# Region attention with keys on partitions, heads in pairs of array tiles, and row maxima only in a branch

## Chip, cores and metric

One core of one Trainium2 chip. The metric is the device time of one execution in microseconds (us), the median of several. A run is fast if it lies within 1.5% of the fastest of its kernel, and only fast runs are compared.

## The reference, cut to what matters

The input is `x`, 4 x 128 channels x 128 x 128. A first layer cuts each image into 9 x 9 overlapping regions of 16 x 16 pixels (step 14) and runs attention with 4 heads of 32 channels within each, then a depthwise 5x5 conv; a second layer has two quantised 3x3 convs. The change touches the attention and the layernorms:

```python
y = _ln(tok, ln1_g, ln1_b)                 # tok: regions x 256 tokens x 128
q, k, v = split(y @ w_qkv)                 # 4 heads of 32
attn = softmax(einsum('bhqd,bhkd->bhqk', q, k) * hd ** -0.5)
o = einsum('bhqk,bhkd->bhqd', attn, v)
tok = o @ w_out + b_out + tok
# overlapping regions are averaged into xf, then
y = _ln(xf, ln2_g, ln2_b) @ w_p0 + b_p0    # 128 -> 256
ym = depthwise_5x5(y); batchnorm; gelu ...
```

## The kernel before

A band is one row of nine regions; there are 36. While band t's attention runs, closures for the projections and second layernorm of band t-1, the first layernorm of band t+1 and the depthwise conv of band t-2 are placed between its steps. A scheduler then orders the instructions of each engine before the run. Scores have queries on partitions: DVE finds row maxima, ACT exponentiates and sums, POOL multiplies by the reciprocal sums, PE transposes, ACT copies, and PE multiplies by the values. Everything in this layer is fp32.

```python
def scores(u):                                   # u: one head of one region
    sc = ps_s.tile([P, 2, NT], F32)
    for c in range(2):
        matmul(sc[:, c, :], qk[hs, 0, c*P:(c+1)*P], qk[hs, 1, :])
    vector.tensor_reduce(nmax, sc, AX.X, ALU.max, negate=True)
    for c in range(2):
        scalar.activation(pr[:, c, :], sc[:, c, :], AF.Exp, bias=nmax[:, c:c+1], accum_out=den[:, c:c+1])
    vector.reciprocal(rden, den)
    for c in range(2):
        gpsimd.tensor_scalar(pr[:, c, :], pr[:, c, :], rden[:, c:c+1], 1.0, ALU.mult, ALU.mult)
def flip(u):    # 4 transposes into pt, then scalar.copy(prt, pt)
def values(u):
    for kc in range(2):
        matmul(po[hs, :], v[:, kc, hs], prt[:, kc, :], start=(kc == 0), stop=(kc == 1))
# step s: scores(s); flip(s - 2); values(s - 3)     39 steps in a band
# ...
side = post_steps(t - 1) if t >= 1 else []          # projections, layernorm 2
side += ln1_steps(t + 1) if t + 1 < T else []       # layernorm 1 of the next band
interleave(attention(t), side, conv_steps(t - 2) if t >= 2 else [])
```

## Time and profile before

| | before |
|---|---|
| median of 3 runs | 7746.85 us (7741.2 to 7783.33) |
| PE / DVE / ACT / POOL busy share of the span | 96 / 68 / 44 / 34% |
| attention stage, then the rest | about 6474 us, then about 1267 us |
| granted PE clock, mean | 0.980 |

The prediction below shows the lines. A busy share says how long an engine worked, not that the span depends on it; here both hold for PE, which is busy 98% of the steady part of the attention stage. The attention stage ends where the second layer's projection starts its first matmul. The "steady part" in this document runs from 360 us to 280 us before that end; the fences show stretches with round ends near it. "Lost clock" is the sum, over the stretches of the steady part in which the profile's clock record grants less than full speed, of their length times the share withheld, whether PE works then or stands. Before it is 73 us.

### The profile page before, as it was taken

What the parts mean: (1) busy time and instruction counts of PE and PEld (TensorE: products, weight loads), DVE (VectorE), ACT (ScalarE), POOL (GpSimd) and SP (SyncE); (2) the same over time, 40 slices, a digit from 0 to 9 for tenths busy, and PEclk for the clock granted to TensorE, in tenths of its full rate; (3) what the DMA queues carried; (4) which work ended last, traced back from release to release, by engine and by line L of the source; (5) the groups of instructions that cost most, each with busy time, mean ns of one, the idle gap of its engine ahead of it and who ended that gap; (6) DMA issues with size and microseconds to landing.
All of it is one profiled execution on the core that took longest, in us unless ns stands there. A gap on an engine that the chain in (4) does not pass through costs nothing.

```text
span 7740.7 us, 86177 instructions
## 1 busy us (share of the span) xinstructions
PE 7448.0 (96%) x28736; PEld 3798.7 (49%) x28736; DVE 5270.3 (68%) x7739; ACT 3438.1 (44%) x8922; POOL 2665.6 (34%) x3443
## 2 busy tenths in 40 slices
PE   8999999999999999999999999999999976999999
PEld 4555555554555555545555555455555532444444
DVE  3467777777677777776777777767777787663333
ACT  4544444443444444434444444444444414661123
POOL 2344444443444444434444444334444411110000
PEclk9999999999999999999999999999999987999999
DMA  0000000000000000000000000000000005870028
GB/s 27 16 28 20 22 20 24 22 24 23 20 20 29 20 22 20 24 22 20 24 22 29 20 22 21 24 20 22 25 22 24 14 23 181 283 245 1 1 78 266
DMA packets 160315, 347.05 MB, mean 45 GB/s; under 512 B 18177, under 2 KB 23937, under 8 KB 155265
## 3 DMA queue, kind: packets, MB, share of 16 engines
q1 hardware_dynamic: 159872, 341.54, 12.6%
q8 instruction: 231, 3.78, 0.2%
q14 instruction: 212, 1.73, 0.1%
HBM read 173.70 MB, written 167.77 MB: 44 GB/s over the span
## 4 chain that ended last, share of the span: by engine, by line
PE 84%; DVE 7%; POOL 4%; ACT 3%; issue 1%; DMA 0%; SPq 0%; DVEq 0%; POOLq 0%; ACTq 0%
PE pm L319 17%; PE sc L390 15%; PE po L430 14%; PE pc L521 10%; PE pt L415 7%; PE pm L372 5%; PE pm L282 4%; DVE acc L330 4%; PE pm L177 3%; PE pm L184 3%; PE pb L569 3%; PE pm L377 2%; PE pm L261 2%; POOL pr L405 2%; POOL xn L192 2%
## 5 line engine op out<-in xcount | busy, mean ns | idle before, releaser
L330 DVE SCALAR_TENSOR_TENSOR acc<-y,dwk,acc 128x1024 f32<-128x1024 f32 (+3 forms) x2736 | 3112.0, 1141 | 21.5
L405 POOL TENSOR_SCALAR pr<-pr,rden 128x256 f32<-128x256 f32 x2592 | 1992.5, 781 | 3086.6 <-DVE rden L403 2368.4
L390 PE MATMUL sc<-qk 32*128 32x256 f32 x5184 | 1467.8, 402 | 14.3 <-ACT pr L398 14.1
L419 ACT COPY prt<-pt 128x512 f32<-128x512 f32 x1296 | 762.4, 588 | 1472.7 <-PE pt L415 1457.9
L319 PE MATMUL pm<-y,diag 128*128 128x512 f32 (+1 forms) x3456 | 1375.5, 551 | 24.9 <-DVE acc L323 24.9
L430 PE MATMUL po<-prt,v 128*32 128x256 f32 x5184 | 1343.9, 388 | 22.4 <-ACT prt L419 22.3
L398 ACT ACTIVATE pr<-sc,nmax 128x256 f32<-128x256 f32 x2592 | 1206.8, 474 | 233.2 <-DVE nmax L394 156.9
L390 PEld LDWEIGHTS sc<-qk 32*128 32x128 f32 x5184 | 860.5, 185 | 778.5 <-issue 367.1
L394 DVE TENSOR_REDUCE nmax<-sc 128x2 f32<-128x512 f32 x1296 | 884.6, 683 | 467.0 <-PE sc L390 461.2
L521 PE MATMUL pc<-q,wq 128*128 128x512 fp8e4 x4608 | 1051.6, 380 | 13.8 <-issue 4.6
L319 PEld LDWEIGHTS pm<-y,diag 128*128 128x128 f32 x3456 | 648.6, 191 | 690.8 <-issue 642.1
L415 PE MATMUL pt<-ident,pr 128*128 128x128 f32 x5184 | 859.0, 286 | 29.0 <-POOL pr L405 25.0
L415 PEld LDWEIGHTS pt<-ident,pr 128*128 128x128 f32 x5184 | 568.6, 141 | 405.6 <-issue 256.7
L521 PEld LDWEIGHTS <-wq 128*128 128x128 fp8e4 x4608 | 447.9, 97 | 648.5 <-issue 157.0
L430 PEld LDWEIGHTS po<-prt,v 128*32 128x32 f32 x5184 | 457.4, 109 | 595.6 <-issue 143.6
L374 ACT COPY qk<-pm 128x512 f32<-128x512 f32 x324 | 189.7, 586 | 1035.7 <-PE pm L372 1035.7
L403 DVE RECIPROCAL rden<-den 128x2 f32<-128x2 f32 x1296 | 209.4, 162 | 600.1 <-ACT pr L398 555.5
L398 ACT ACTIVATION_READ_ACCUMULATOR pr<-sc,nmax 128x1 f32 x2592 | 530.1, 205 | 0.0
L323 DVE SCALAR_TENSOR_TENSOR acc<-y,dwk,pm 128x512 f32<-128x512 f32 (+1 forms) x288 | 197.6, 686 | 407.1 <-PE pm L319 407.1
L372 PE MATMUL pm<-yr,wqkv 128*128 128x256 f32 x1296 | 382.7, 410 | 37.7 <-POOL yr L192 37.7
L282 PE MATMUL pm<-xn,wp 128*128 128x512 f32 (+1 forms) x576 | 299.6, 648 | 31.5 <-POOL xn L192 22.5
L569 PE MATMUL pb<-ge,wp 128*128 128x512 f32 x512 | 253.3, 599 | 68.9 <-ACT ge L566 68.9
(86 smaller groups left out, 5032.1 us busy)
## 6 DMA issues: line engine op xcount, KB each, us to landing
cv<-cv_d SPq DMA_DIRECT2D x128, 512.0 KB, 4.3
cv_d<-acc SPq DMA_DIRECT2D x80, 512.0 KB, 2.9
xt<-in_x_dram SPq DMA_DIRECT2D x36, 1024.0 KB, 5.1
xfl<-xf_d SPq DMA_DIRECT2D x128, 256.0 KB, 3.2
id_d<-y SPq DMA_DIRECT2D x128, 256.0 KB, 2.6
idt<-id_d SPq DMA_DIRECT2D x128, 256.0 KB, 3.2
out_dram<-z SPq DMA_DIRECT2D x128, 256.0 KB, 2.5
xf_d<-xf SPq DMA_DIRECT2D x112, 256.0 KB, 2.0
```

The lines of the kernel that those rows point to most:

```text
L282: nc.tensor.matmul(pm[:, : n * P], wp0[:, h, :], held["xn"][:, : n * P], start=True, stop=True)
L319: nc.tensor.matmul(pm[:, :n, :], diag[:, h, k, :], tap(h, k, r, n), start=(k == 0), stop=(k == PE_TAPS - 1),)
L330: nc.vector.scalar_tensor_tensor(a, tap(h, k, g, gn), dwk[:, h, k : k + 1], a, ALU.mult, ALU.add)
L372: nc.tensor.matmul(pq[:, m, :], wqkv[:, m * P : (m + 1) * P], y, start=True, stop=True)
L390: nc.tensor.matmul(sc[:, c, :], qk[hs, 0, c * P : (c + 1) * P], qk[hs, 1, :], start=True, stop=True)
L394: nc.vector.tensor_reduce(nmax, sc, AX.X, ALU.max, negate=True)
L398: nc.scalar.activation(pr[:, c, :], sc[:, c, :], AF.Exp, bias=nmax[:, c : c + 1], accum_out=den[:, c : c + 1],)
L405: nc.gpsimd.tensor_scalar(pr[:, c, :], pr[:, c, :], rden[:, c : c + 1], 1.0, ALU.mult, ALU.mult)
L415: nc.tensor.transpose(pt[:, kc, c * P : (c + 1) * P], pr[:, c, kc * P : (kc + 1) * P], ident)
L419: nc.scalar.copy(prt, pt)
L430: nc.tensor.matmul(po[hs, :], v[:, kc, hs], prt[:, kc, :], start=(kc == 0), stop=(kc == 1))
L521: nc.tensor.matmul(pc, w[:, t, :], q[:, k * RB + dy : k * RB + dy + RB, dx : dx + P], start=(t == 0), stop=(t == 8),)
```

## The change

Its intent: compute the scores transposed, so that the keys are on partitions and the exponentials are at once the operand of the values matmul. That removes the transposes and their copies. The sums over keys, now over partitions, come from a matmul with ones; the division goes to the output. Without row maxima the exponential needs a bound on the scores, so a flag is computed from the weights and a branch holds the general form with maxima (not taken for these inputs). Heads go in pairs, whose matmuls lie in different tiles of the PE array. Gains and biases of the layernorms are folded into weights.

```diff
+    with tc.If(flag > 0): front(False)
+    with Else: front(True)             # with row maxima
 def scores(u):                         # u: now a pair of heads
-    vector.tensor_reduce(nmax, ...); Exp with bias and accum_out; reciprocal; gpsimd.tensor_scalar x2
+    sc = ps_s.tile([P, 2, 2, NT], F32)
+    for c in range(2):
+        for a in range(2):             # two heads, two row tiles
+            matmul(sc[:, a, c, :], qk[hs, 1, c*P:(c+1)*P], qk[hs, 0, :])
+    scalar.activation(pr, sc, AF.Exp)                                  # 1024 elements
+    gpsimd.tensor_tensor(both, pr[:, :, 0, :], pr[:, :, 1, :], ALU.add)
-def flip(u): ...
 def values(u):
+    for c in range(2):
+        for a in range(2):             # two column tiles
+            matmul(po[hs, 0, :], v[:, c, hs], pr[:, a, c, :], start=(c == 0), stop=(c == 1))
+    for a in range(2):
+        matmul(po[hs, 1, :], ones[:, hs], both[:, a, :])
+    # after the second pair: rden = exp(-ln(sums)) on ACT, product and overlap add on DVE
 # layernorm tail
-    vector.tensor_tensor(xh, pc, rstd, ALU.mult); gpsimd.tensor_scalar(o, xh, g, bias, ...)
+    # in its head: vector.tensor_copy(xc, pc)
+    gpsimd.tensor_tensor(o, xc, rstd, ALU.mult)
 # q,k out of PSUM
-    scalar.copy(qk, pq)
+    vector.tensor_tensor(qk, pq, bqk broadcast, ALU.add)
 # steps of a band
-    scores(s); flip(s - 2); values(s - 3)      # 39 steps
+    scores(s); values(s - 1)                   # 19 steps
 # PSUM banks
-    ps_s 2 x 1, ps_t 2 x 1, ps_o 1, ps_m 3
+    ps_s 2 x 2, ps_o 2, ps_m 2
```

## The prediction

> **What bounds the kernel now.** I read four views in this order: the page's busy table and slices, the stretches, the groups by line with shapes kept apart, and the timeline of one stretch.
>
> ```profile
> span 7740.7 us, 86177 instructions
> PE 7448.0 (96%) x28736; PEld 3798.7 (49%) x28736; DVE 5270.3 (68%) x7739; ACT 3438.1 (44%) x8922; POOL 2665.6 (34%) x3443
> ...
> PE 84%; DVE 7%; POOL 4%; ACT 3%; issue 1%; DMA 0%; SPq 0%; DVEq 0%; POOLq 0%; ACTq 0%
> ```
>
> ```profile
> 360.00:6280.00 5920.00, 5792.02 (x22124) 3038.70 (x22124) 4372.56 (x6237) 2721.92 (x7749) 2460.38 (x3064) 0.99 0.06 22
> 6280.00:6480.00 200.00, 93.54 (x200) 43.17 (x198) 182.84 (x200) 16.58 (x22) 9.59 (x20) 0.69 0.11 40
> ```
>
> The columns of the stretches are busy us of PE, PEld, DVE, ACT and POOL, then the granted clock. In the attention stage (to about 6480 us) PE is busy 98% of the steady stretch, DVE 74%, ACT 46%, POOL 42%. Only the last 180 us of the stage belong to DVE, which finishes the depthwise conv there. The remaining 1260 us are stages that the change doesn't touch. So PE's time in the attention stage is what counts, and the first question is where it goes.
>
> ```profile
> L390 PE MATMUL sc<-qk 32*128 32x256 f32 x5184 | 1467.8, 402 | 14.3 <-ACT pr L398 14.1
> L430 PE MATMUL po<-prt,v 128*32 128x256 f32 x5184 | 1343.9, 388 | 22.4 <-ACT prt L419 22.3
> L415 PE MATMUL pt<-ident,pr 128*128 128x128 f32 x5184 | 859.0, 286 | 29.0 <-POOL pr L405 25.0
> ```
>
> ```profile
> 3006.86 0.66 PE L415 MATMUL pt<-ident,pr 128*128 128x128 f32 x4
> 3007.45 1.05 PE L430 MATMUL po<-prt,v 128*32 128x256 f32 x4
> 3008.43 1.13 PE L390 MATMUL sc<-qk 32*128 32x256 f32 x4
> 3009.48 0.66 PE L415 MATMUL pt<-ident,pr 128*128 128x128 f32 x4
> ...
> 167.76 1.14 PE L390 MATMUL sc<-qk 32*128 32x256 f32 x8
> ```
>
> Two things are to be seen. One head costs 3009.48 - 3006.86 = 2.62 us of PE when nothing else comes between (four transposes 0.59, four value records 0.98, four score records 1.05). An fp32 matmul is two records here: 2592 score matmuls make 5184. And the last line is the key to the change: where scores of two heads happen to stand together, x8 takes 1.14 us, as long as x4. In the single records there, the two heads start 13 ns apart and proceed in step, 0, 13, 320, 333, 535, 549, 751, 765 ns. Two row tiles really run side by side in fp32. Two value groups side by side do the same (0, 14, 240, 254, 456, 470, 672, 685 ns), but such starts are rare now: 10 pairs of score records and 99 of value records.
>
> **What the Trainium skill says.** "TensorEngine Tiling (Array Packing)", Key Properties: different tiles execute independently, and changing the tiling mode drains the engine. The trace agrees with both: the 13 ns starts, and a record spacing of 216 ns within a score group against 305 to 309 ns where the shape of the tile changes. "SBUF — State Buffer", Who interferes with whom: a VectorE instruction with two SBUF inputs and a GpSimd instruction that reads SBUF exclude each other, and the second waits for the whole of the first. The trace agrees: the normalisation of probabilities on POOL takes 478 ns alone and 1503 ns when it starts inside a depthwise tap. "GPSIMD Engine Reference", 3.1: a two-input fp32 add of 2048 elements takes 4497 ns on GpSimd. This trace has no large two-input POOL instruction, so I scale to 512 elements and estimate 1.17 us from that page. "ScalarE: Activation LUTs", What ACT_TABLE_LOAD costs: 0.833 ns an element. The trace agrees: copies of 256 and 512 take 378 and 586 to 588 ns.
>
> **The change on PE.** A pair of heads has 4 score matmuls (8 records) in two row tiles, so 4 slots: 320 + 216 + 216 + 305 = 1.06 us. Values are 4 matmuls and the sums by ones 2 more, 12 records in two column tiles, 6 slots: 240 + 4 x 216 + 309 = 1.41 us. Transposes are gone. The pair costs 2.47 us in place of 2 x 2.62 = 5.24. Counting from the start of each PE record to the next one's, the three groups now take 1393 + 1280 + 835 = 3508 us of the stage's 6453 (some waits and mixing included). New: 648 pairs x 2.47 = 1600. PE saves 1908 and needs 6453 - 1908 = 4545 us. The last number still holds the conv tail.
>
> **The change on ACT and POOL.** ACT loses the transposed copies (762), the read-outs of sums (530), the q,k copies (190) and 2592 exponentials (1207). It gains 648 exponentials of 1024 elements at about 1.01 us (588 + 512 x 0.83 ns), 655 us, and ln and exp of the sums, 324 x (0.38 + 0.42) = 260. It falls to some 1.7 ms, and is no bound. POOL loses 1992 us of normalisation and gains 648 adds of the two key halves, 1.17 us alone; the 224 large layernorm scalings become two-input, too. With the waits for the shared port I expect 1.8 to 2.4 ms, no bound either. A step of one pair takes about 7 us, and exp plus add need 3 to 4, which the lag of one step covers.
>
> **The change on DVE.** In the stage it is now busy: taps 3116 (the 2736 of one line), first taps 198, statistics 172, residual 99, overlap add 135, layernorm product 180, row maxima 885, reciprocals 209, together 4994. Removed: maxima, reciprocals and layernorm product, 1274. Added: copy of the centred values out of PSUM (224 x 0.68 + 64 x 0.42 = 180), q,k bias (324 x 0.69, the shape of the layernorm product, = 222), scaling of the output by the reciprocal sums (324 x 0.42 = 135). New: 4994 - 1274 + 537 = 4257. On top comes the shared port. A 128x1024 tap that no POOL instruction overlaps takes 1.277 us, the overlapped ones 1.333, and all the taps lose only 82 us now, because POOL's pieces are 0.48 us and some 0.24 us of one hides under the next tap's start. A POOL add of 1.17 us that slips in between two taps delays the next by about 0.93 us. Of the 648 + 288 two-input POOL instructions I let 600 fall so (560 us, rounded down to 550 with the rest ignored). DVE: 4257 - 82 + 550 = 4725 us, **more than PE's 4545**. So the bound goes over from PE to DVE.
>
> **The sum.** DVE can't be full throughout. The first two bands have no conv; at 84 us each ((4545 - 1452) / 36, 1452 being the conv matmuls) it idles some 120 us. In-order waits for PE and ACT, 1.7 ms in total today beside a full PE, I put at 200. The stage: 4725 + 120 + 200 = 5045, that is 1408 less than 6453. The fold of gains, the bound for the scores and the branch stand before the first layernorm and let nothing overlap: 40 us, a guess. 7747 - 1408 + 40 = 6380. One risk has a direction: the score tiles double, so the general PSUM pool falls from three buffers to two, and q,k and the centred values are now evacuated by the full DVE instead of ACT. For PE stalls that come back as DVE waits I add 70: **6450 us**.
>
> **The rivals.**
> - *Serial tiles.* If the heads of a pair don't overlap in the new order, a pair needs 8 + 12 records of 216 ns and two switches, 4.7 us: PE saves only 3508 - 648 x 4.7 = 460, remains the bound at about 6.0 ms, and the kernel takes some 7300 us. Against it: the in-step starts above, and that the built program alternates heads within each group.
> - *PSUM starvation.* With two buffers PE waits for DVE at layernorm, q,k and conv. Some 29 evacuations of a band are DVE's; one us of PE stall each, 36 x 29 = 1040, makes a stage of 5590 and 6920 us in all. For it: DVE's queue is always full then. Against it: the centred copy frees its buffer sooner than the product did, which waited for the reciprocal root.
> - *Little contention on the port.* If POOL's adds mostly run beside DVE's PSUM work, DVE needs 4300, PE's 4545 bounds, and 200 us of waits give a stage of 4750 and 6090 us in all.
>
> **Range and chances.** PE and DVE come out so close that either error alone moves the time by a few hundred us; the floor is PE's 4545 (about 5880 in all) with no wait anywhere, which I don't believe. 8 in 10: 6150 to 6850. Even with serial tiles the kernel is faster by over 2%; slower needs starvation far beyond 1 us each, so faster 0.95, same 0.03, slower 0.02.
>
> **What would show it.** PE: score and ones/value records of a pair starting within some 20 ns of each other, and about 1.6 ms busy in these three groups. DVE: over 90% busy in the steady stretch, and first in the chain that ended last, with taps whose mean has risen by some 0.2 us. POOL: adds of about 1.2 us alone, near 2 with waits. ACT: exponentials of about 1.0 us. PE's largest waits should be for DVE's evacuations of the general PSUM tiles. The prediction is wrong if PE is still 95% busy with few pairs in step (serial tiles), or if both PE and DVE show idle of over 15% in the steady stretch (starvation or a chain across POOL that I took as covered).

## The result and the profile after

The changed kernel takes 6951.09 us (median of 4 runs, 6946.71 to 6957.91) against 7759.8 in the same rounds: ratio 0.8962, interval 0.8939 to 0.8985. A ratio here is the mean time of the one kernel's fast runs over the mean of the other's of the same rounds, so not quite the ratio of the medians. It is faster, but 101 us beyond the range's end.

From the page of the changed kernel: busy times, the first part of the chain, and the groups of attention and of the taps.

```profile
span 6948.2 us, 67884 instructions
PE 6218.0 (89%) x26166; PEld 2973.3 (43%) x26166; DVE 5183.4 (75%) x5815; ACT 2227.2 (32%) x3423; POOL 1821.1 (26%) x1502
...
PE 60%; DVE 22%; issue 9%; POOL 6%; ACT 3%; SPq 0%; DMA 0%; POOLq 0%; ACTq 0%; DVEq 0%
...
L387 DVE SCALAR_TENSOR_TENSOR acc<-y,dwk,acc 128x1024 f32<-128x1024 f32 (+3 forms) x2736 | 3580.9, 1315 | 42.4
L484 POOL TENSOR_TENSOR both<-pr 128x512 f32<-128x512 f32 x648 | 1031.5, 1592 | 2815.8 <-ACT pr L482 2687.8
L472 PE MATMUL sc<-qk 32*128 32x256 f32 x5184 | 1034.0, 427 | 17.8 <-DVE qk L433 17.8
L497 PE MATMUL po<-pr,v 128*32 128x256 f32 x5184 | 722.2, 388 | 0.0
L500 PE MATMUL po<-both,ones 128*32 128x256 f32 x2592 | 408.0, 380 | 0.8 <-POOL both L484 0.8
```

The steady stretch of the changed kernel, in the columns that the prediction explains:

```profile
360.00:5480.00 5120.00, 4583.42 (x19384) 2234.80 (x19384) 4255.04 (x4348) 1557.30 (x2551) 1606.80 (x1226) 0.92 0.07 25
```

Here is the riddle: PE is busy 90%, DVE 83%. Neither engine is full, and PE's clock fell from 0.99 to 0.92. What they wait for is in the waits of PE (longest in total first; columns: waited for, us in total, times, longest us):

```profile
PE pm L431 <- POOL yr L252: 240.6, 36, 7.9
PE pm L339 <- POOL xn L252: 196.9, 74, 7.7
PE pb L645 <- ACT ge L642: 70.7, 4, 67.7
PE pm L239 <- DVE xc L243: 33.9, 30, 1.2
```

The first is a wait in 36 bands: the q,k projection of a band's first region needs `yr`, the first layernorm of that band. The second is the same kind of wait at the projection after the second layernorm. In the kernel before, the q,k projection's wait was 37.7 us:

```profile
PE pm L372 <- POOL yr L192: 37.7, 32, 3.6
```

One of these waits in the timeline (start, duration, engine; the lines of four engines, sorted by engine):

```profile
3145.15 0.70 PE L239 MATMUL pm<-xt,center 128*128 128x256 f32 x2 [1.23 <-DVE xc L243]
3146.32 0.70 PE L248 MATMUL pm<-sq,avg 128*128 128x256 f32 x2 [0.47 <-ACT sq L241]
3153.03 2.07 PE L431 MATMUL pm<-yr,wqkv 128*128 128x256 f32 x4 [6.01 <-POOL yr L252]
...
3147.62 0.42 ACT L251 ACTIVATE rstd<-rstd 128x256 f32<-128x256 f32 x1
...
3145.02 4.15 DVE L387 SCALAR_TENSOR_TENSOR acc<-y,dwk,acc 128x512 f32<-128x512 f32 x4
3149.09 0.42 DVE L506 TENSOR_TENSOR on<-po,rden 128x256 f32<-128x256 f32 x1
3149.42 0.74 DVE L387 SCALAR_TENSOR_TENSOR acc<-y,dwk,acc 128x512 f32<-128x512 f32 x1
3150.08 0.42 DVE L508 TENSOR_TENSOR ob<-on,ob 128x256 f32<-128x256 f32 x1
3150.42 0.42 DVE L243 COPY xc<-pm 128x256 f32<-128x256 f32 x1
...
3150.93 0.84 POOL L294 TENSOR_SCALAR ob<-ob 128x256 f32<-128x256 f32 x1
3151.74 1.24 POOL L252 TENSOR_TENSOR yr<-xc,rstd 128x288 f32<-128x288 f32 x1
```

PE has centred the last two rows by 3145.85. ACT has their reciprocal root at 3148.04. But the copy of the centred values stands in DVE's queue behind five taps, a product (L506) and an overlap add (L508) and runs at 3150.42; POOL's product can only then follow, behind another POOL instruction. PE stands until 3153.03, and what comes then runs slowly: four records take 2.07 us there, and 1.13 us where the clock is full. The stretches around it show the clock (seventh quantity):

```profile
3130.00:3146.00 16.00, 14.60 (x82) 5.97 (x80) 15.68 (x20) 8.06 (x14) 7.33 (x8) 1.00 0.04 16
3146.00:3153.00 7.00, 0.70 (x2) 0.30 (x2) 6.20 (x9) 1.16 (x3) 3.49 (x5) 0.60 0.00 1
3153.00:3163.00 10.00, 9.97 (x30) 6.93 (x31) 3.49 (x5) 1.77 (x3) 2.71 (x6) 0.60 0.08 28
```

Counted over the trace, the steady part has 80 stretches of lower clock (31 before) and 403 us of lost clock (73 before). The page "TensorE: Matmul & The Clock Gate" of the Trainium skill, Part 1, says that idle gaps of more than some 3.4 us halve the clock and that it takes as much busy time to come back. The trace agrees that the clock is halved: its record has no other values than 1.0 and 0.5. The way back took longer here: after the 34 gaps at `yr`, 7.0 us long on the mean, PE's clock stayed low for 3.4 to 13.1 us, 9.3 on the mean, though PE was busy 96% of that time.

The third finding is in the order of records. Pairs do run in step: where the eight score records of a pair stand together they start at 0, 10, 320, 330, 540, 540, 750, 760 ns (rounded). But that holds for 293 of 648 pairs. The scheduler put other matmuls between the rest: there are 438 groups of 2 score records, 188 of 4 and 196 of 6, in all 1118 groups for 648 pairs.

### The profile page after: what moved, and what is told of

The parts are those of the page before. It is cut to its first block, busy times and chain, and to the rows that moved or that the text cites. A ratio compares the mean times of both kernels' runs of the same rounds, so it can differ in the third digit from the quotient of the medians.

```text
span 6948.2 us, 67884 instructions
## 1 busy us (share of the span) xinstructions
PE 6218.0 (89%) x26166; PEld 2973.3 (43%) x26166; DVE 5183.4 (75%) x5815; ACT 2227.2 (32%) x3423; POOL 1821.1 (26%) x1502
## 4 chain that ended last, share of the span: by engine, by line
PE 60%; DVE 22%; issue 9%; POOL 6%; ACT 3%; SPq 0%; DMA 0%; POOLq 0%; ACTq 0%; DVEq 0%
PE pm L376 16%; DVE acc L387 15%; PE pc L597 12%; PE sc L472 7%; PE po L497 5%; PE pm L431 4%; PE pm L339 4%; PE pb L645 3%; POOL both L484 2%; POOL xn L252 2%; PE pm L438 2%; PE po L500 2%; PE pm L318 2%; PE pm L248 1%; ACT a L672 1%
## 5 line engine op out<-in xcount | busy, mean ns | idle before, releaser
L387 DVE SCALAR_TENSOR_TENSOR acc<-y,dwk,acc 128x1024 f32<-128x1024 f32 (+3 forms) x2736 | 3580.9, 1315 | 42.4
L484 POOL TENSOR_TENSOR both<-pr 128x512 f32<-128x512 f32 x648 | 1031.5, 1592 | 2815.8 <-ACT pr L482 2687.8
L482 ACT ACTIVATE pr<-sc 128x1024 f32<-128x1024 f32 x648 | 663.8, 1024 | 1515.0 <-PE sc L472 1502.3
L472 PE MATMUL sc<-qk 32*128 32x256 f32 x5184 | 1034.0, 427 | 17.8 <-DVE qk L433 17.8
L472 PEld LDWEIGHTS sc<-qk 32*128 32x128 f32 x5184 | 538.4, 192 | 674.6 <-issue 536.6
L497 PE MATMUL po<-pr,v 128*32 128x256 f32 x5184 | 722.2, 388 | 0.0
L431 PEld LDWEIGHTS pm<-yr,wqkv 128*128 128x128 f32 x1296 | 260.2, 220 | 403.6 <-POOL yr L252 257.1
L500 PE MATMUL po<-both,ones 128*32 128x256 f32 x2592 | 408.0, 380 | 0.8 <-POOL both L484 0.8
L497 PEld LDWEIGHTS po<-pr,v 128*32 128x32 f32 x5184 | 249.4, 109 | 344.4 <-issue 167.5
L248 PE MATMUL pm<-sq,avg 128*128 128x512 f32 (+1 forms) x576 | 307.4, 616 | 38.1 <-ACT sq L241 24.6
```

The costliest lines, as they stand in the source:

```text
L248: nc.tensor.matmul(pv[:, :n], avg, held["sq"][:, :n], start=True, stop=True)
L387: nc.vector.scalar_tensor_tensor(a, tap(h, k, g, gn), dwk[:, h, k : k + 1], a, ALU.mult, ALU.add)
L431: nc.tensor.matmul(pq[:, m, :], wqkv[:, m * P : (m + 1) * P], y, start=True, stop=True)
L472: nc.tensor.matmul(sc[:, a, c, :], qk[hs, 1, c * P : (c + 1) * P], qk[hs, 0, :], start=True, stop=not general,)
L482: nc.scalar.activation(pr, sc, AF.Exp)
L484: nc.gpsimd.tensor_tensor(both, pr[:, :, 0, :], pr[:, :, 1, :], ALU.add)
```

## The experiments

Theories for the 500 us between 6450 and 6951: *chain* (PE stands at short in-order chains through DVE's queue, ACT and POOL, and its clock falls after it); *DVE* (as predicted, DVE with the port that it shares with POOL is the bound, only more so); *PSUM* (two general buffers hold PE up). All kernels gave correct results. Times are medians; "PE busy", "DVE busy" are shares of the steady part. PE's time there splits without rest into three terms: PE idle; "withheld while busy", the part of the lost clock that falls on a busy PE; and PE's work as it would be at full clock. The split is by kind of time, not by cause.

### The order of the steps: a1, a2, a3

```diff
 # a1
-side = post_steps(t - 1); side += ln1_steps(t + 1)
+side = ln1_steps(t + 1); side += post_steps(t - 1)
 # a2: scores and values of a pair as steps of their own, 38 in a band
-steps.append(step)
+steps += [step, second]
 # a3: both
```

> Only the order of the side work of a band is changed: the layernorm of the next band goes before the projections of the previous one. Chain theory (at the end of a band PE stands some 7 us for the last rows of the next band's layernorm, which pass through the end of a full DVE queue and through POOL, and runs at half clock for some 10 us after that): PE's wait for yr falls from 240 us to under 40, the lost clock from 418 us to about 200, time 6951 to 6550-6700. DVE theory (DVE with the shared port is the bound, as predicted, and PE's waits cost nothing): within 1% of 6951. PSUM theory (two general buffers hold PE up): within 2%.

> Only the interleaving is finer: scores and values of a pair are steps of their own, so a band has 38 main steps in place of 19 and the layernorm's links fall into different steps. Chain theory: PE's wait for xn at the first projection (197 us, 2 to 3 us each) falls by half or more, the wait for yr at the band's end stays or falls a little, time 6951 to 6750-6880. DVE and PSUM theory: within 1%.

> Both of the changes of the two other runs. Chain theory: PE's waits for yr and xn together from 437 to under 120 us, granted clock of the steady stretch from 0.92 to 0.97 or more, time 6400-6600; then DVE is above 88% busy in the steady stretch. DVE theory: within 1% of 6951.

| | time | ratio to before, interval | PE idle us | lost clock us | withheld while busy us | PE work at full clock us | PE / DVE busy |
|---|---|---|---|---|---|---|---|
| changed kernel | 6951 | 0.896 (0.894 to 0.899) | 524 | 403 | 281 | 4235 | 90 / 83% |
| a1 layernorm 1 first | 6574 | 0.846 (0.843 to 0.850) | 327 | 137 | 123 | 4215 | 93 / 90% |
| a2 finer steps | 6758 | 0.870 (0.867 to 0.874) | 377 | 299 | 273 | 4202 | 92 / 87% |
| a3 both | 6566 | 0.845 (0.842 to 0.849) | 337 | 121 | 106 | 4200 | 93 / 91% |

The longest wait of PE in a1 (the wait for `yr` is no longer in its list):

```profile
PE pm L339 <- POOL xn L252: 143.3, 104, 8.3
```

Moving a few closures took 377 us off with the same instructions. That refutes the DVE theory for the changed kernel: a full DVE could not have given 377 us. It supports the chain theory: of what a1 gained, 197 us are idle time of PE, 158 clock withheld from a busy PE, and 20 work. The finer steps gave 193 us alone; on top of a1 only 8 us, within what rounds differ by: they cure the same wait (80 us of it are left in a2). The expectations for the `xn` wait missed: a2 asked for half of 197 us and has 169, a3 asked for `yr` and `xn` together under 120 us and has 183 for `xn` alone; a1, which asked for nothing there, has 143.

### Is the clock a cost of its own: a4, a5

```diff
 # before the first q,k projection of a band; a4 has 8, a5 has 5
+keep = ps_m.tile([P, 512], F32, name="pm")
+for _ in range(8):
+    matmul(keep, center, xb[t][:, 0:4, :])      # result not used
```

> Eight useless fp32 matmuls of 512 columns (about 6.8 us) stand before the first q,k projection of a band, where PE waits for yr. They add work on PE and shorten no chain. If the lower clock after the wait is a cost of its own, the clock stays up at the band's start, the lost clock falls from 418 to about 250 us, and the time falls by 50 to 150 us although PE does 240 us more work. If the wait alone costs and the clock hardly matters, the time is equal or up to 1% longer.

> The clock question again, with five useless matmuls (4.3 us) ahead of the first q,k projection of a band, because the eight overran the gap by 2.0 us a band on the mean and were no clean test. If the lower clock after the gap is a cost of its own: lost clock 403 to 300 us or less and 30 to 120 us faster than 6951. If it only accompanies the gap: equal within 0.5%.

a4 took 7055 us, 104 more than the changed kernel: a miss. The eight matmuls ended 2.0 us after `yr` was there, on the mean (4 to 5 us in some bands), so they lengthened the chain that they should have filled, and lost clock fell only to 287 us. a5 was the clean form: in most bands the projection starts 54 ns after `yr`. It took 6906 us, 45 us less than the changed kernel, although PE did 116 us more work in the steady part; lost clock 265 us. So the lower clock costs time by itself: idle time of PE went into dummy work, and 37 of the 45 us are clock no longer withheld from a busy PE. The gain is small beside 377, as the dummies only fill the gap and don't remove it.

### Is the reordering simply better, and what is pairing worth: c4, d1, d2

```diff
 # c4: the kernel BEFORE with a1's edit
 # d1: the changed kernel, the pair torn apart on PE
-scores(s); values(s - 1)
+for a in range(2):          # one head of the pair at a time
+    scores(s, a); values(s - 1, a)
 # d2: the kernel BEFORE, two heads side by side (cut: a fourth buffer in the pool attn_t, and the place of the q,k projection's call)
-scores(s); flip(s - 2); values(s - 3)
+scores(s); scores(s + 1); | flip(s - 2); flip(s - 1); values(s - 4); values(s - 3)
```

> Control: the kernel before with the layernorm of the next band ahead of the projections, the edit that took 377 us off the changed kernel. PE was 98% busy there, so all theories say within 1% of before; the chain theory says that the wait for yr (38 us) goes and no more than 60 us in all.

> The changed kernel with the two heads of a pair torn apart on PE: scores of one head, then values and sums of one head, then the other head; the work is the same instruction for instruction. If the side-by-side tiles are worth what the prediction took (10 slots of 216 ns and two mode switches of a pair, 2.6 us, 648 pairs), PE needs about 1690 us more and is the bound again: 7800 to 8400 us, slower than the kernel before. If the scheduler or the engine overlaps them anyway: 7000 to 7200.

> The kernel before, with row maxima and transposes kept, but with scores and values of two heads put next to each other on PE. If pairing alone carries the gain: PE saves up to 8 slots of 216 ns a pair and a part of the switches, up to 1100-1400 us, so 6500-6900 us. If ACT's, DVE's and POOL's chain through maxima, exponentials and normalisation then holds PE up: 7000 to 7500. If the transposes were the larger part, or the tiles overlap only where the instructions alternate: over 7500.

c4 took 7995 us, ratio 1.029 (1.027 to 1.032): slower, where all theories said equal. Its steady part is 257 us longer: 153 us are clock withheld from a busy PE, 63 idle, 41 work. PE's wait for POOL's probabilities grew from 25 to 91 us and that for ACT's exponentials from 14 to 53. The new order gives PE more short waits in the attention itself; why the clock falls so far with them is not shown. So a1's order is no general improvement; the same edit costs a PE-bound kernel 3% and gives the changed one 5%.

d1 took 7558 us (2 runs): tearing the pairs costs 607 us. In the steady part PE's work grew by 1195 us (1690 expected for pairs torn without exception), while PE's idle time fell by 409 and the clock withheld by 175. The expected 7800 was missed, because the scheduler put some heads together again (410 score records start within 60 ns of the one before, 1964 in the changed kernel). PE is full again and its clock stays up:

```profile
360.00:6000.00 5640.00, 5524.15 (x19425) 2690.02 (x19424) 4143.16 (x4331) 1562.82 (x2555) 1482.84 (x1222) 0.98 0.06 23
```

d2 took 7781 us (2 runs), ratio 1.001 (0.999 to 1.004): pairing in the kernel before gave nothing. Its tiles do run in step: 3447 of the score and value records start within 60 ns of the one before, and those two groups hold PE for 1201 + 758 us in place of 1393 + 1280 (from start to next start). In the steady part PE's work fell by 861 us, but clock withheld from a busy PE grew by 527 us and idle time by 372. PE, DVE, ACT and POOL are busy for 92, 72, 44 and 42% of the stretch below, so no engine is full; the waits that grew are those for POOL's probabilities and for the same two layernorm tiles:

```profile
360.00:6220.00 5860.00, 5375.48 (x21609) 2934.88 (x21607) 4199.16 (x6068) 2598.98 (x7575) 2480.26 (x2994) 0.89 0.06 22
...
PE pt L415 <- POOL pr L405: 200.3, 282, 1.2
PE pm L372 <- POOL yr L192: 149.1, 36, 4.7
PE pm L282 <- POOL xn L192: 137.0, 99, 7.9
```

Lost clock is 649 us, and the transposes hold PE for 1133 us (835 before). Of the expectations, the number over 7500 came, but not for the reasons given with it, as the tiles do overlap. Whether it would have gained with another order wasn't tried; this run shows only that shorter PE groups alone didn't shorten this stage. It is the same in kind as what befell the change: saved work came back as waits and low clock.

### The shared port and the balance: c1, d3, d4

```diff
 # c1: a3 without POOL's add
-gpsimd.tensor_tensor(both, pr[:, :, 0, :], pr[:, :, 1, :], ALU.add)
-matmul(po[hs, 1, :], ones[:, hs], both[:, a, :])
+for c in range(2):
+    matmul(po[hs, 1, :], ones[:, hs], pr[:, a, c, :], start=(c == 0), stop=(c == 1))
 # d3: c1 with one depthwise tap moved from PE to DVE; d4: with two
-PE_TAPS = 6
+PE_TAPS = 5        # d4: 4
```

> The reordered kernel of a3 without POOL's add of the two key halves: the ones matmul runs over both halves and accumulates. It takes 648 large two-input instructions off the port that POOL shares with DVE, and adds 4 records in two tiles (2 slots, 0.43 us) to a pair, 280 us of PE. Port theory: the taps fall from a mean of 1.341 us to under 1.22, DVE's busy time by 300 us or more. Which bound: if DVE holds the reordered kernel, 6566 falls by 100 us or more; if PE does, it rises by 100 to 280.

> Reordered, without POOL's add, and with one depthwise tap moved from PE to DVE. PE was 97% busy in that kernel without the move and DVE 82%: a tap is 3456/6 = 576 records of PE, some 245 us, and 144 tap instructions of DVE, some 170 us. If PE is the bound there: 6566 to 6320-6430. If the kernel hangs on chains instead: within 1% of 6566.

> The same with two taps moved: PE 490 us less than without the move, DVE some 340 us more, which brings DVE to about 4150 us busy against some 4050 of PE. If the two bounds meet: no better than one tap moved, 6300 to 6450.

c1 took 6566 us, as a3 did, so neither expectation for the time came. Yet the engines changed places: the taps' mean fell from 1.341 to 1.175 us, DVE from 91 to 82% busy, and PE rose to 97%:

```profile
360.00:5000.00 4640.00, 4495.23 (x21457) 2234.37 (x21456) 3786.52 (x4258) 1558.77 (x2513) 581.17 (x616) 0.99 0.07 28
```

So the adds cost the taps 0.166 us x 2736 = 455 us, where the prediction had 550 for adds and layernorm products together. Taking them away was worth nothing by itself: in the steady part PE took on 270 us of work, and its idle time fell by 190 and the clock withheld by 63. With DVE's room, moving work off PE pays: d3 took 6390 (0.821, 0.820 to 0.823), 176 us less than c1; d4 6360 (0.817, 0.816 to 0.819), 30 us less again, where DVE's 89% and PE's 93% meet.

### Buffers and the link in DVE's queue: b2, e1, e2, and the fastest: e3, e4

```diff
 # b2: the changed kernel; e2: a1; e3: d3
-ps_o 2, ps_m 2
+ps_o 1, ps_m 3
 # e1: the changed kernel; e4: d4
-nc.vector.tensor_copy(xc[:, :n], pc[:, :n])
+nc.scalar.copy(xc[:, :n], pc[:, :n])
```

> The changed kernel with three general PSUM buffers in place of two, paid for with one output accumulator in place of two. PSUM theory (PE is held up because two buffers drain through a full DVE queue): 6951 falls by 100 us or more and PE's waits for yr and xn fall, too. Chain theory (the waits are for POOL's results of a short in-order chain, whatever the buffers): within 1.5% of 6951, waits for yr and xn within 20% of 437 us; the single accumulator may cost up to 100 us.

> The changed kernel with one edit: the copy of the centred values out of PSUM is ACT's, not DVE's. If DVE's full queue is the long link at the band's end, PE's wait for yr falls from 240 us to under 130 and that for xn from 197 to under 150, and the time by 150 to 300 us (of which 180 of DVE work could count only if DVE were the bound). If the order of the steps alone makes the wait: within 1% of 6951.

> Layernorm first, and three general PSUM buffers. If the two gains (377 and 141 us) are separate: 6574 to about 6430. If the third buffer only helped PE around the same wait, or the single output accumulator costs as much: within 1% of 6574.

> The version with one tap moved (6390) with three general PSUM buffers: 6270 to 6350 if fewer torn score groups save PE what they saved in the changed kernel, over 6390 if values, which now wait for the single accumulator, cost more.

> The version with two taps moved (6360) with the centred copy on ACT: DVE loses some 180 us of work, PE's wait for xn (216 us) falls by a third or more. 6150 to 6290 if either counts there; 6330 or more if PE's own work is the bound.

b2 took 6810 us, 141 less: the time that the PSUM theory asked for. Its waits point both ways. Those for `yr` and `xn` fell from 437 to 360 us, which is 18% and so within what the chain theory allowed, new ones for the single accumulator came, and PE was idle as long as before (547 us, 524 in the changed kernel):

```profile
PE pm L431 <- POOL yr L252: 183.0, 35, 6.2
PE pm L339 <- POOL xn L252: 176.8, 87, 8.8
PE po L497 <- DVE on L506: 138.4, 101, 3.9
```

What fell is PE's busy time, from 4517 to 4366 us, with the number of score groups: 874 in place of 1118. The third buffer let the scheduler keep more pairs whole. The traces say where the time went: PE's work in the steady part fell by 196 us, while idle time grew by 21 and clock withheld by 44. Over the whole stage the work fell by 203 us, and the score records have 118 of them. So more than half of the gain in work lies in the scores, with their fewer torn groups; the rest is spread over values (22), sums (19) and others.

e1 took 6839 us, 112 less, with the wait for `yr` down from 241 to 95 us (under 130 expected) and that for `xn` not at all (212; under 150 expected). So the copy's place in DVE's queue is a real link of the chain, and worth about a third of what the order of steps gives: PE's idle time fell by 111 us, its work and its clock stayed. At least 150 us were expected. e2 took 6550, 24 less than a1 (0.843 against 0.846, the intervals meet): the third buffer's gain and the reordering's don't add up, as the waits for the accumulator grow to 273 us there.

e3 took **6255 us** (0.805, 0.803 to 0.806), with e4 the fastest, and a little under the 6270 expected: layernorm first, finer steps, no POOL add, five taps on PE, three general buffers. It beats the kernel before by 19.5% and the changed one by 10%:

```profile
360.00:4700.00 4340.00, 4091.11 (x20932) 2068.59 (x20930) 3905.66 (x4387) 1543.55 (x2509) 618.37 (x612) 0.98 0.08 29
```

e4 took 6265 us (0.806), 95 less than d4 and level with e3 within what rounds differ by. Its time was expected, its wait was not: the one for `xn` fell from 216 to 180 us, not by a third.

## Why the prediction was wrong

- **PE's side of a pair, 2.47 us: right where it is whole.** Eight score records 1.06 us, eight value records 0.89, four sums 0.53: 2.48. Over the stage it was not: at full clock the three groups are 921 + 596 + 359 = 1876 us of work, not 1600, and most of the excess is in the torn score groups (648 whole pairs would take 648 x 1.06 = 687 us). From start to next start, with waits and low clock, they take 1147 + 603 + 417 = 2167 us. The 3508 us of the old groups were of this second kind too, so the saving of 1908 mixed waits into work: PE's work in the stage fell from 6106 to 4659 us, by 1447.
- **DVE's sum, 4725 us: its terms right but one, the total too high as a busy time.** Copies took 0.682, q,k 0.687 and products 0.418 us each, as taken from the old rows; the overlap add took 0.61 instead of 0.42, which was not foreseen (62 us). The taps came to 3581 (3584 predicted: 3116 - 82 + 550), in part by luck: 600 delays of 0.93 us were assumed, and 725 taps took over 150 ns more than the fastest of their shape, 0.78 us more on the mean; the longest took 2.38 us. But the sum adds durations, and DVE's instructions overlap by some 80 ns each: in the stage before, durations of 5037 us are 4684 us busy (5270, less 586 after the stage), and in the changed kernel 4838 are 4597. By the same share the prediction's 4725 is an estimated 4490 us busy, which lies *below* the 4545 of PE. So the crossing of the bound to DVE rests on two measures that can't be compared.
- **ACT and POOL: right.** Exponentials 1.024 us (1.01 predicted), POOL's adds 1.59 us on the mean and 1.27 where no tap lies beside them (1.17 estimated); POOL 1821 us in all, at the lower end of 1.8 to 2.4 ms.
- **The step that failed: "In-order waits for PE and ACT ... I put at 200", and with it the bound.** With two engines nearly level I took the larger sum for the bound and let its waits be small. DVE stood idle for 865 us of the steady stretch and 1084 of the whole stage, where 120 + 200 were allowed, and 70 more for buffers. The prediction had said that a lag of one step covers the chain exp and add, and that is so (PE waited 0.8 us for the sums' operand). It did not look at the other chain, the layernorm's, whose links the change moved into DVE's and POOL's queues, while it halved the steps of a band, so that there is less attention work between two links and none left at a band's end. That chain stopped PE for 437 us (the waits for `yr` and `xn`), and clock withheld from a busy PE rose from 70 to 281 us. Putting the layernorm first gave back 377 of the 501 us by which the prediction was short, and a3, where PE and DVE are both over 90% busy, lies at 6566, inside the range. The prediction's own last sentence named the sign, both engines idle, though at over 15%; PE's idle share is 10%.
- **The added 70 us for buffers** were of another kind: the third buffer was worth 141 us in the changed kernel and 24 after the reordering, and not through waits for DVE's evacuations, which the rival made 1040 us. That rival's 6920 is close to the measured time for the wrong reason.
- **Serial tiles** are refuted by the trace, and d1 shows what that would cost.
- What stays open: how the 501 us divide by cause. The traces split the stage by kind (before: 271 us idle, 97 withheld while busy, 6106 work; after: 709, 313 and 4659), but a run that removes one cause changes the others. Open too are why the clock fell in c4, and the wait for `xn`: among the variants of the changed kernel only d1, whose PE is full, has less than 113 us (28).

## What to carry to other kernels

When a change takes a third off the bounding engine, don't only ask which busy sum is the largest next: list the chains that pass through several in-order queues, and ask what work is left beside each. Work that used to hide a chain is gone with the time saved, and a TensorE that stood for 7 us on the mean ran at half clock for 9 us after it here. When two engines come out nearly level, compare busy times, not sums of durations: here the estimated busy times stood in the other order. Where such a chain shows, look first at the order of the closures, which is cheap to change: here it was worth nearly half as much as the whole change, but the same order cost the old kernel 3%.

## What the Trainium skill lacked or had wrong

- "TensorE: Matmul & The Clock Gate", Part 3, says that matmuls start and end strictly in program order. In d2 the program has two score matmuls of one head, then two of the other; in 213 groups the eight records start at 0, 10, 320, 330, 540, 550, 750, 760 to 770 ns. If the built order is also the order in which PE gets them, which no run here shows, the second head's first record starts before the first head's second.
- The same page, Part 1, lets the clock return after some 3.4 us of sustained work. Here it returned 3.4 to 13.1 us after the gaps at `yr`, 9.3 on the mean, with PE busy 96% of the time between.
- "TensorEngine Tiling (Array Packing)", Key Properties, names the drain at a change of mode without a cost: 305 to 309 ns between records where 216 is the stream, so some 90 ns each.
- Neither page has fp32 among its packing figures: two fp32 row tiles gave 8 records in 1.06 us, 4 records alone take 1.06, so the full factor of two.
- "GPSIMD Engine Reference", 3.1, gives the two-input add for 2048 elements only. For 512 its slope gave an estimate of 1.17 us; the trace has 1.27 us alone and 1.59 on the mean beside DVE.
- "SBUF — State Buffer", Who interferes with whom, was right in kind (without POOL's adds, in c1, the taps fell from 1.341 to 1.175 us). It gives no measure of how often the two engines meet: here 725 of 2736 taps took over 150 ns more than the fastest of their shape, 0.78 us more on the mean.
